# Layer norms of the MLP and of the image attention: the variance by one product with a matrix of ones, the reciprocal over all partitions

## The chip, the core and the metric

The kernel runs on one core of a Trainium2 chip. The time is the device time of one execution, in microseconds (us). The core has five engines that work side by side, each in the order of its own queue: PE (matrix products), DVE (elementwise work and reductions), ACT (functions of one argument, copies), POOL (elementwise work, a slower second one) and SP (issues DMAs). They wait for one another by semaphores. Products land in PSUM, which has eight banks of 128 partitions x 512 numbers; everything else lies in SBUF, 128 partitions wide.

## What is computed

Four images of 56 x 56 positions (L = 3136) and 128 channels pass four layers; each layer reads the group norm of x and is added to x. Layers 0 and 3 are the ones the change touches:

```python
x = x + _L0_conv_ref(_gn(x), ...)      # attention block
x = x + _L1_conv_ref(_gn(x), ...)      # selective scan
x = x + _L2_conv_ref(_gn(x), ...)      # deformable convolution
x = x + _L3_conv_ref(_gn(x), ...)      # attention block

# inside an attention block
attn_wins = _mha(wins, wq, bq, wk, bk, wv, bv, wo, bo)      # windows of 7 x 7
...
xf = xf + _mha(_layernorm(xf, g1, be1), wq, bq, wk, bk, wv, bv, wo, bo)
h = jax.nn.gelu(_layernorm(xf, g2, be2) @ w1 + b1, approximate=False)
xf = xf + (h @ w2 + b2)

def _layernorm(x, g, b, eps=1e-05):
    m = jnp.mean(x, axis=-1, keepdims=True)
    v = jnp.mean((x - m) ** 2, axis=-1, keepdims=True)
    return (x - m) * jax.lax.rsqrt(v + eps) * g + b
```

All of it is fp32. The two layer norms, over the 128 channels of each position, are the subject.

## The kernel before

Channels lie on the partitions and positions along the free axis, so an image is a tile of 128 x 3136. Work goes by chunks of 448 positions; an image has seven (NCK). One core does the four images one after the other, and each image has two attention blocks, so each stage below runs eight times. Inside these stages the order of the instructions is written out by hand: every engine takes its instructions in the order in which the loop issues them. The tiles' framework adds the waits and deals out the PSUM banks.

**The layer norm of a chunk.** A sum over channels is a sum over partitions, which is work for PE. `ln_center` (L140) multiplies the chunk by (identity - 1/128) and leaves the centred chunk in PSUM (`ln_pc`). ACT squares it into `ln_sq`. `ln_spread` (L150) takes the square in four pieces of 112 positions as the stationary side and a column of 1/128 as the moving side, so that the variances come out across 112 partitions, four to each (`ln_pv`); ACT takes the root of 112 x 4 numbers and DVE the reciprocal (`ln_rs`). `ln_rows` (L162) brings them back: four products of a broadcast column with the identity give 128 x 448 in PSUM, the same row in every partition (`ln_pb`), and ACT copies it to SBUF. DVE multiplies the centred chunk by it (`scale`), and ACT applies gain and bias (`shift`, an Identity). The scan's layer norm uses `ln_spread` too, with two halves of channels, and is not touched.

**First stage of the attention** (`attention`, loop over u = 0 to 8). The windowed attention of band u (tokens, project, queries, keys, values, scores, exponentials, normalize, turn, turned, weigh, out) is interleaved with the layer norm of chunk u - 2 and with `inputs`, which makes k, q and v of the image attention from it. Between them stand four calls of `some`, each four products of q with k (L349) and four maxima of them on DVE (L350) for the first four query blocks, if such work is ready. Of the names that the prediction uses: L302 is the eviction of `out`, L235 and L241 those of the queries (q) and keys (kb), L247 the copy of the values (v), L267 the exponential, L281 and L286 the transposes and their copies (turn, turned), L383 the square, L392 scale, L395 shift, L400 and L401 the products for k and q and their evictions. A pool of eight PSUM banks serves all of this.

**The image attention itself** (from L429 on) is long and not touched; its sums are inverted by L593, reciprocals of 128 x 112. It uses `one32`, a tile of ones of 128 x 32.

**The MLP** (`mlp`). Seven chunks again, in a loop over n from -1: `residual` (product with wo, L653, and DVE's add, L654), `center` (with POOL's add of x, L660), `spread`, `scale`, `shift`, `hidden` (four products, L679, and four Gelus, L680), `result` (four products, L686) and `store` (DVE's add, L690, then the statistics for the next group norm, L115, or in layer 3 `finish`, which sends the chunk out by DMA and fetches the next image's). In a turn, the norm of chunk n + 1 stands between the two halves of chunk n's `hidden`, and the residual of n + 2 follows. The pool has eight banks. Gelu, the root and the exponential lie in different function tables of ACT; a change of table is an instruction of its own (ACT_TABLE_LOAD).

Of the kernel before, what the change touches and what calls it, by code (L numbers as in the profile page):

```python
# [10 lines left out]
F32 = mybir.dt.float32  # L11
F32R = mybir.dt.float32r
I32 = mybir.dt.int32
AF = mybir.ActivationFunctionType
# [5 lines left out]
P = 128  # L20
HW = 56
L = HW * HW
CH = 448
NCK = L // CH
NH = 4
DK = P // NH
# [6 lines left out]
NPR = BAND // PW  # L33
# [37 lines left out]
def _offsets(cols):  # L71
    at, n = {}, 0
    for name, w in cols:
        at[name] = (n, w)
        n += w
    return at, n


class _Net:
    def __init__(self, ctx, tc, x, packs, out):  # L80
        self.tc, self.nc, self.x_in, self.out = tc, tc.nc, x, out
        self.B = x.shape[0]
        nc = self.nc
        wp = ctx.enter_context(tc.tile_pool(name="weights", bufs=1))
        self.keep = wp
        self.w = {}
        for i, (layer, cols) in enumerate(COLS.items()):
            at, n = _offsets(cols)
            t = wp.tile([P, n], F32, tag=f"w_{layer}", name=f"w_{layer}")
            (nc.sync if i % 2 == 0 else nc.scalar).dma_start(t, packs[layer])  # L90
            self.w[layer] = {name: t[:, o : o + k] for name, (o, k) in at.items()}
        c = self.w["C"]
        self.ident, self.gmat = c["ident"], c["gmat"]
        self.ones = {1: c["ones1"], 2: c["ones2"]}
        self.center = {1: (c["center1"],), 2: (c["center2"], c["others2"])}
        self.sel = wp.tile([P, KB], F32R, tag="sel", name="sel")
        nc.vector.memset(self.sel.bitcast(F32), 0.0)
        for h in range(NH):
            nc.vector.memset(self.sel[h * DK : h * DK + 2, :].bitcast(F32), 1.0)
        self.ident2 = wp.tile([64 + NX, NX], F32R, tag="ident2", name="ident2")  # L100
        nc.vector.memset(self.ident2.bitcast(F32), 0.0)
        for k in (0, 64):
            nc.vector.tensor_copy(self.ident2[k : k + NX, :], self.ident[:NX, :NX])
        self.one32 = wp.tile([P, DK], F32, tag="one32", name="one32")
        nc.vector.memset(self.one32, 1.0)
        self.eps = wp.tile([P, 1], F32, tag="eps", name="eps")
        nc.vector.memset(self.eps, 1e-5)
        self.x = wp.tile([P, L], F32, tag="x", name="x")
        self.st = wp.tile([P, NCK, 6], F32, tag="gn_st", name="gn_st")
        self.dpool = ctx.enter_context(tc.tile_pool(name="tables", bufs=1, space=DRAM))  # L110
# [51 lines left out]
    def ln_rows(self, dst, rs, bank):  # L162

        nc, k = self.nc, rs.shape[1]
        pb = bank("ln_pb")
        for i in range(k):
            nc.tensor.matmul(pb[:, i * QB : (i + 1) * QB], lhsT=rs[:, i : i + 1].to_broadcast([QB, P]), rhs=self.ident[:QB, :QB], start=True, stop=True)
        nc.scalar.copy(dst, pb[:, : k * QB])


    def swin_prepare(self, layer):
# [25 lines left out]
    def windows(self, layer, x, x1, gn, sb, bank):  # L197
# [5 lines left out]
        nc, w = self.nc, self.w[layer]  # L203
# [9 lines left out]
        def keep(name, t, shape):  # L213
            later[name, t] = sb.tile([P] + shape, F32, tag=name, name=name)
            return later[name, t]
# [27 lines left out]
        def values(t):  # L243
            pv = bank("pv")
            for r in range(NPR):
                nc.tensor.matmul(pv[:, r * P : (r + 1) * P], lhsT=xw[t % 2][:, 2 * r : 2 * r + 2, :].rearrange("p j k -> p (j k)"), rhs=w["wv"], start=True, stop=True)
            nc.vector.tensor_copy(keep("v", t, [NPR * P]), pv)  # L247

        def scores(t):
            s, m = keep("s", t, [ng, n1]), keep("m", t, [ng])  # L250
# [56 lines left out]
    def attention(self, layer, x, x1, oT, sb):  # L307
# [9 lines left out]
        nc, tc, w = self.nc, self.tc, self.w[layer]  # L317
# [8 lines left out]
        def part(c):  # L326
            return slice(c * CH, (c + 1) * CH)
# [12 lines left out]
        with tc.manual_schedule():  # L340
# [33 lines left out]
            with tc.tile_pool(name="ap_sb", bufs=2) as tb, tc.tile_pool(name="ap_ps", bufs=8, space=PSUM) as ps:  # L374
                bank = lambda name: ps.tile([P, 512], F32, tag="mm", name=name)
                of_windows = self.windows(layer, x, x1, self.group_norm(tb, ps), tb, bank)
                nc.gpsimd.memset(kl, 0.0)
                ln = {}
# [5 lines left out]
                    ln[c] = pc, sq  # L384

                def spread(c):
                    ln[c] += (self.ln_spread(ln[c][1][:, 0:1, :], bank, tb),)

                def scale(c):
                    pc, sq, rs = ln[c]  # L390
                    self.ln_rows(sq[:, 1, :], rs, bank)
                    nc.vector.tensor_mul(sq[:, 0, :], pc[:, :CH], sq[:, 1, :])  # L392

                def shift(c):
# [23 lines left out]
                def some():  # L418
                    if groups:
                        i, kc = groups.pop(0)  # L420
                        for h in range(NH):
                            maximum(i, h, kc, mx0[home[i][0]], bank, part(kc))

                def do(name, t):

                    if name in of_windows:
                        if 0 <= t < NWIN:
                            of_windows[name](t)
                    elif 0 <= t < NCK:  # L429
                        {"center": center, "spread": spread, "scale": scale, "shift": shift, "inputs": inputs}[name](t)  # L430

                for name in ("tokens", "project", "queries", "keys", "values"):
                    do(name, 0)
                do("tokens", 1)
                for u in range(NWIN + 1):
                    if u != 1:
                        do("scores", u)
                    do("out", u - 1)
                    some()
                    do("tokens", u + 2)  # L440
                    if u != 1:
                        do("exponentials", u)
                    do("center", u - 2)
                    if u != 1:
                        do("normalize", u)
                    do("project", u + 1)
                    do("spread", u - 2)
                    do("queries", u + 1)
                    do("values", u + 1)
                    if u == 0:  # L450
                        for name in ("keys", "scores", "exponentials", "normalize"):
                            do(name, 1)
                    some()
                    do("scale", u - 2)
                    if u != 0:
                        do("keys", u + 1)
                    some()
                    do("turn", u)
                    do("shift", u - 2)
                    do("turned", u)  # L460
                    do("inputs", u - 2)
                    some()
                    do("weigh", u)
# [10 lines left out]
            with tc.tile_pool(name="at_sb", bufs=2) as tb, tc.tile_pool(name="at_ps", bufs=2, space=PSUM) as ps:  # L474

                bank = lambda name: ps.tile([P, 512], F32, tag="mm", name=name, bufs=7)
# [123 lines left out]
                for g in range(ng + 8):  # L600
                    qc, k = divmod(g, NKB)
# [37 lines left out]
    def mlp(self, layer, x, x1, oT, last):  # L639


        nc, tc, w = self.nc, self.tc, self.w[layer]
        with tc.tile_pool(name="mlp", bufs=2) as sb, tc.tile_pool(name="mlp_ps", bufs=8, space=PSUM) as ps, tc.manual_schedule():
            bank = lambda name: ps.tile([P, 512], F32, tag="mm", name=name)
            x2, m = x1, {}

            def cols(n):
                c = (n + 3) % NCK
                return slice(c * CH, (c + 1) * CH)

            def residual(n):
                py = bank("py2")
                nc.tensor.matmul(py[:, :CH], lhsT=w["wo"], rhs=oT[:, n * CH : (n + 1) * CH], start=True, stop=True)  # L653
                nc.vector.scalar_tensor_tensor(x2[:, cols(n)], py[:, :CH], w["boe"], x1[:, cols(n)], ALU.add, ALU.add)  # L654

            def center(n):
                (m["pc", n],) = self.ln_center([x2[:, cols(n)]], bank)
                m["sq", n] = sb.tile([P, 2, CH], F32, tag="ln_sq", name="ln_sq")
                nc.scalar.activation(m["sq", n][:, 0, :], m["pc", n][:, :CH], AF.Square)
                nc.gpsimd.tensor_add(x2[:, cols(n)], x2[:, cols(n)], x[:, cols(n)])  # L660

            def spread(n):
                m["rs", n] = self.ln_spread(m["sq", n][:, 0:1, :], bank, sb)

            def scale(n):
                sq = m["sq", n]
                self.ln_rows(sq[:, 1, :], m.pop(("rs", n)), bank)
                nc.vector.tensor_mul(sq[:, 0, :], m.pop(("pc", n))[:, :CH], sq[:, 1, :])

            def shift(n):  # L670
# [25 lines left out]
            def do(f, n, *args):  # L696
                if 0 <= n < NCK:
                    f(n, *args)

            residual(0)  # L700
            for n in range(-1, NCK):
                do(center, n + 1)
                do(hidden, n, (0, 1))
                if n < 0:
                    residual(1)
                do(spread, n + 1)
                do(hidden, n, (2, 3))
                do(residual, n + 2 if n >= 0 else -1)
                do(scale, n + 1)
                do(result, n)  # L710
                do(shift, n + 1)
                do(store, n)


# [773 lines left out]
```

## Time and profile before

| | us |
|---|---|
| median of 3 timed runs | 13458.64 (13451.59 to 13462.05) |
| the profiled execution, its own time | 13245.72 |
| its span, first to last instruction | 13243.9 |
| mean granted PE clock | 0.933 |
| first stage of the attention, from the first scores (L257) to the eighth, first block | 29.50 to 150.69 |
| MLP, first L654 to last L690, eight of them | 69.56 to 74.65 |

The profiled execution is one run of its own, about 213 us below the timed median; durations are read from it. Of the operations that the change removes or alters, in the whole program:

| line, engine | operation | count | mean ns |
|---|---|---|---|
| L156 PE | variance, 128x112 by one column | 896 in the two norms (two records each product) | 237 (median) |
| L158 ACT | root, 112x4 | 140, with the scan's | 263 |
| L159 DVE | reciprocal, 112x4 | 140, with the scan's | 178 |
| L167 PE | back to rows, 112x112 | 896 | 298 |
| L168 ACT | copy, 128x448 | 112 | 532 |
| L247 DVE | copy of v, 128x512 | 64 | 684 |

A timeline line gives the start, the time that the merged instructions cover, the engine, the line, the operation with output and input, the count, and in brackets how long the engine stood idle before and what released it. PE works on an fp32 product in two records.

### The profile page before, as it was taken

The page shows a single profiled execution, that of the slowest core. Times are in us where ns is not written, and L with a number is a line of the kernel's source. Part 1 is how long each engine was busy: PE and PEld are TensorE (multiplying, and loading weights), DVE is VectorE, ACT ScalarE, POOL GpSimd, SP SyncE. Part 2 cuts the span into 40 slices and gives each one's busy share as a digit, 9 for nine tenths or more (in the row PEclk, how much of TensorE's full clock was granted, in tenths as well). Part 3 has the DMA queues.
Part 4 walks back from the last instruction along what each step waited for, and adds up shares of the span by engine and source line. Part 5 has one row for each costly group of instructions (what it writes and reads, how often), then busy time and mean ns, then how long its engine had stood idle before and what let it go on. Part 6 is the DMA issues. An engine that isn't in the chain of part 4 may idle for free. (4 is left out here: it accounts for less than half of the span.)

```text
span 13243.9 us, 218251 instructions
## 1 busy us (share of the span) xinstructions
PE 11713.7 (88%) x85716; PEld 7459.5 (56%) x85716; DVE 9575.5 (72%) x11831; ACT 7563.6 (57%) x19130; POOL 9941.6 (75%) x6852
## 2 busy tenths in 40 slices
PE   8999995699898999579989899957999989995799
PEld 4448884444544888444454488834445448883444
DVE  6649996665665999666466499966646649996664
ACT  5567772356556777235655677723565567772356
POOL 4949995488494999548849499954975949995497
PEclk9999997799999999779999999977999999996799
DMA  2000004200000000420000000042000000004200
GB/s 100 1 14 4 5 4 118 78 1 6 6 1 14 4 5 4 120 75 1 8 4 1 14 5 5 4 125 70 1 9 2 1 14 5 5 4 130 65 1 6
DMA packets 181178, 344.60 MB, mean 26 GB/s; under 512 B 20104, under 2 KB 101416, under 8 KB 180024
## 3 DMA queue, kind: packets, MB, share of 16 engines
q0 software_dynamic: 80640, 231.28, 6.3%
q1 hardware_dynamic: 99224, 97.83, 2.4%
q8 instruction: 678, 11.11, 0.4%
q14 instruction: 348, 2.85, 0.1%
q10 hardware_dynamic: 288, 1.53, 0.0%
HBM read 256.04 MB, written 74.52 MB: 25 GB/s over the span
## 5 line engine op out<-in xcount | busy, mean ns | idle before, releaser
L555 POOL TENSOR_TENSOR es<-es,e 128x896 f32<-128x896 f32 x2016 | 4158.8, 2088 | 133.0 <-ACT e L549 75.0
L350 DVE TENSOR_REDUCE mx<-pm 128x1 f32<-128x512 f32 (+1 forms) x4928 | 3056.5, 670 | 1411.1 <-PE pm L349 795.8
L549 ACT ACTIVATE e<-pst 128x448 f32<-128x448 f32 (+1 forms) x5600 | 2677.6, 544 | 1893.3 <-PE pst L547 1348.1
L1066 DVE TENSOR_TENSOR_SCAN hs<-da,dbu 128x928 f32<-128x928 f32 x1792 | 3633.0, 2070 | 53.2 <-ACT dbu L1059 29.3
L1075 POOL TENSOR_TENSOR hs<-hs,cb 128x896 f32<-128x896 f32 x1792 | 3486.9, 1963 | 26.0 <-ACT carry L1070 20.8
L349 PE MATMUL pm<-ks,qs 32*128 32x512 f32 (+1 forms) x9856 | 2911.8, 636 | 13.4 <-DVE nm L371 7.8
L547 PE MATMUL pst<-qs,ks 32*128 32x448 f32 x11200 | 2685.4, 547 | 0.0
L1084 PE MATMUL yt<-w_C,hs 128*116 128x128 f32 x14336 | 1865.8, 273 | 1.1 <-POOL hs L1075 1.1
L542 PE MATMUL pst<-nm,sel 32*128 32x448 f32 x5600 | 1638.7, 614 | 0.0
L1084 PEld LDWEIGHTS yt<-w_C,hs 128*116 128x116 f32 x14336 | 1570.5, 135 | 2.1 <-POOL hs L1075 2.1
L1048 PE MATMUL dbu<-dgb,ut 112*128 112x224 f32 x7168 | 1258.5, 298 | 268.8 <-DVE hs L1066 268.7
L571 PE MATMUL po<-e,va 128*32 128x448 f32 (+1 forms) x11200 | 1352.4, 551 | 0.1
L349 PEld LDWEIGHTS pm<-ks,qs 32*128 32x128 f32 x9856 | 924.3, 186 | 745.2 <-DVE mx L350 618.9
L1325 POOL DMA_INDIRECT g<-tab,idx x1008 | 940.5, 933 | 452.9 <-issue 425.8
L1048 PEld LDWEIGHTS dbu<-dgb,ut 112*128 112x128 f32 x7168 | 945.3, 192 | 534.2 <-DVE hs L1066 524.2
L1002 ACT ACTIVATE da<-dl,A 128x112 f32<-128x112 f32 x3584 | 1194.6, 383 | 0.1
L547 PEld LDWEIGHTS pst<-qs,ks 32*128 32x128 f32 x11200 | 1098.0, 185 | 102.6 <-issue 13.7
L1351 PE MATMUL pvt<-w_C,g 112*128 112x112 f32 x2016 | 404.5, 367 | 729.3 <-issue 607.8
L542 PEld LDWEIGHTS pst<-nm,sel 32*128 32x128 f32 x5600 | 570.6, 184 | 740.2 <-DVE mx L350 387.1
L1352 ACT COPY vt<-pvt 128x336 f32<-128x336 f32 x336 | 147.2, 438 | 1188.0 <-PE pvt L1351 1184.5
L1351 PEld LDWEIGHTS pvt<-w_C,g 112*128 112x128 f32 x2016 | 315.2, 203 | 823.1 <-issue 784.2
L1070 ACT COPY carry<-hs 128x32 f32<-128x32 f32 x1792 | 397.5, 222 | 623.3 <-DVE hs L1066 615.2
(230 smaller groups left out, 15791.4 us busy)
## 6 DMA issues: line engine op xcount, KB each, us to landing
tab<-zero SPq DMA_DIRECT2D x4, 6728.0 KB
g<-tab,idx POOLq DMA_INDIRECT x1008, 3.5
tab<-gt SPq DMA_DIRECT2D x32, 448.0 KB
dl_d<-dl SPq DMA_DIRECT2D x28, 448.0 KB
dl<-dl_d SPq DMA_DIRECT2D x56, 224.0 KB
tab<-gt SPq DMA_DIRECT2D x32, 336.0 KB
out_dram<-x SPq DMA_DIRECT2D x28, 224.0 KB
x<-in_x_dram SPq DMA_DIRECT2D x21, 224.0 KB
```

Of the source, the lines that this page charges most:

```text
L349: nc.tensor.matmul(pm[:, :m], lhsT=qs[head(h), q.start : q.start + P], rhs=ks[head(h), keys], start=True, stop=True)
L350: nc.vector.tensor_reduce(mx[:, home[i][1], h, kc : kc + 1], pm[:, :m], AX.X, ALU.max)
L542: nc.tensor.matmul(t[:, :CH], lhsT=self.sel[head(h), :], rhs=nm[head(h), part(qc)], start=True, stop=False)
L547: nc.tensor.matmul(t[:, :CH], lhsT=ks[head(h), k * KB : (k + 1) * KB], rhs=qs[head(h), part(qc)], start=False, stop=True)
L549: nc.scalar.activation(e[:nk, j, :], t[:nk, :CH], AF.Exp, scale=SCALE)
L555: nc.gpsimd.tensor_tensor(s, es[g - 1, p][:nk] if k == 1 else s, e[:nk], ALU.add)
L571: nc.tensor.matmul(m["po"][head(h), :CH], lhsT=va[:nk, k, head(h)], rhs=src(h)[:nk], start=(k == 0), stop=(k == NKB - 1))
L1002: nc.scalar.activation(m["da"][:, :, n, 2:], dl(), AF.Exp, scale=A[:, j, n : n + 1])
L1048: nc.tensor.matmul(pu[:, 8 * h : 8 * h + 8, 2 + tb * TB : 2 + (tb + 1) * TB], lhsT=made[g]["ut", 2 * r + tb][:, d, :], rhs=made["r", g // ...
L1066: nc.vector.tensor_tensor_scan(flat(pairs[u // 2][:, d % 2]), flat(made[g]["da"][:, r]), flat(banks.pop(u)), 0.0, ALU.mult, ALU.add)
L1075: nc.gpsimd.tensor_tensor(hs, hs, made["r", g // 2]["cb"][:, :, r * HW : (r + 1) * HW], ALU.mult)
L1084: nc.tensor.matmul(sums[q][:YR, e * P : (e + 1) * P], lhsT=hs[:, n, :], rhs=self.ident, start=(n == 0), stop=(n == NST // 2 - 1), is_trans ...
```

## The change

A tile of ones of 128 x 128 (`all1`) takes the place of `one32`, which becomes a slice of it. The new `ln_root` multiplies the square by it: one product of 128x128 by 128x448 puts the sum over channels of every position into every partition, and ACT takes the root of the whole 128 x 448 from PSUM, with 1/128 as scale and eps as bias. DVE then inverts 128 x 448 numbers. In the image attention this is in two halves (`invert0`, `invert1`) with a call of `some` between them, and the copy of v goes from DVE to ACT. In the MLP it is one reciprocal, and the loop's order is changed: centre, variance and reciprocal are a chunk further ahead, the residual two chunks further, and the first of these stand ahead of the loop.

```diff
-        self.one32 = wp.tile([P, DK], F32, tag="one32", name="one32")
-        nc.vector.memset(self.one32, 1.0)
+        self.all1 = wp.tile([P, P], F32, tag="all1", name="all1")
+        nc.vector.memset(self.all1, 1.0)
+        self.one32 = self.all1[:, :DK]
...
+    def ln_root(self, dst, sq, bank):
+
+        pv, k = bank("ln_pv"), sq.shape[-1]
+        self.nc.tensor.matmul(pv[:, :k], lhsT=self.all1, rhs=sq, start=True, stop=True)
+        self.nc.scalar.activation(dst, pv[:, :k], AF.Sqrt, bias=self.eps, scale=1.0 / P)
...
-            nc.vector.tensor_copy(keep("v", t, [NPR * P]), pv)
+            nc.scalar.copy(keep("v", t, [NPR * P]), pv)
...
                 def spread(c):
-                    ln[c] += (self.ln_spread(ln[c][1][:, 0:1, :], bank, tb),)
+                    sq = ln[c][1]
+                    self.ln_root(sq[:, 1, :], sq[:, 0, :], bank)
+
+                def invert(c, i):
+                    r = ln[c][1][:, 1, i * (CH // 2) : (i + 1) * (CH // 2)]
+                    nc.vector.reciprocal(r, r)
 
                 def scale(c):
-                    pc, sq, rs = ln[c]
-                    self.ln_rows(sq[:, 1, :], rs, bank)
+                    pc, sq = ln[c]
                     nc.vector.tensor_mul(sq[:, 0, :], pc[:, :CH], sq[:, 1, :])
...
                     do("spread", u - 2)
                     do("queries", u + 1)
                     do("values", u + 1)
+                    do("invert0", u - 2)
                     if u == 0:
                         for name in ("keys", "scores", "exponentials", "normalize"):
                             do(name, 1)
                     some()
+                    do("invert1", u - 2)
                     do("scale", u - 2)
...
             def spread(n):
-                m["rs", n] = self.ln_spread(m["sq", n][:, 0:1, :], bank, sb)
+                sq = m["sq", n]
+                self.ln_root(sq[:, 1, :], sq[:, 0, :], bank)
+                nc.vector.reciprocal(sq[:, 1, :], sq[:, 1, :])
 
             def scale(n):
                 sq = m["sq", n]
-                self.ln_rows(sq[:, 1, :], m.pop(("rs", n)), bank)
                 nc.vector.tensor_mul(sq[:, 0, :], m.pop(("pc", n))[:, :CH], sq[:, 1, :])
...
             residual(0)
+            residual(1)
+            center(0)
+            residual(2)
+            spread(0)
             for n in range(-1, NCK):
-                do(center, n + 1)
                 do(hidden, n, (0, 1))
-                if n < 0:
-                    residual(1)
-                do(spread, n + 1)
+                do(scale, n + 1)
+                do(center, n + 2)
                 do(hidden, n, (2, 3))
-                do(residual, n + 2 if n >= 0 else -1)
-                do(scale, n + 1)
+                do(shift, n + 1)
+                do(residual, n + 4)
+                do(spread, n + 2)
                 do(result, n)
-                do(shift, n + 1)
                 do(store, n)
```

More of the change, by code (lines that the diff above doesn't have):

```diff
@@ L429, in do @@
                     elif 0 <= t < NCK:
-                        {"center": center, "spread": spread, "scale": scale, "shift": shift, "inputs": inputs}[name](t)
+                        {
+                            "center": center, "spread": spread, "invert0": lambda c: invert(c, 0), "invert1": lambda c: invert(c, 1),
+                            "scale": scale, "shift": shift, "inputs": inputs,
+                        }[name](t)
                 for name in ("tokens", "project", "queries", "keys", "values"):
```

## The prediction

> **What bounds the kernel now.** I read the page's busy shares first, then the timelines of the two stages that the change touches, then the rows of single operations.
>
> ```profile
> PE 11713.7 (88%) x85716; PEld 7459.5 (56%) x85716; DVE 9575.5 (72%) x11831; ACT 7563.6 (57%) x19130; POOL 9941.6 (75%) x6852
> ```
>
> The share of PE is an average; the touched stages differ. There are eight of each: four images, two attention blocks (L0, L3). A turn of the MLP's loop, PE alone, in the timeline (start, duration, engine, line):
>
> ```profile
> 834.13 0.92 PE L147 MATMUL ln_pc<-x,w_C 128*128 128x448 f32 x2
> 834.88 1.67 PE L679 MATMUL ph<-xn,w_L 128*128 128x448 f32 x4
> ...
> 836.39 0.85 PE L156 MATMUL ln_pv<-w_C,ln_sq 128*112 128x1 f32 x8
> ...
> 837.10 1.75 PE L679 MATMUL ph<-xn,w_L 128*128 128x448 f32 x4
> ...
> 838.69 0.92 PE L653 MATMUL py<-oTi,w_L 128*128 128x448 f32 x2
> ...
> 839.44 1.04 PE L167 MATMUL ln_pb<-w_C,ln_rs 112*128 112x112 f32 x8
> ...
> 840.32 3.19 PE L686 MATMUL py<-h,w_L 128*128 128x448 f32 x8
> ...
> 843.34 0.92 PE L147 MATMUL ln_pc<-x,w_C 128*128 128x448 f32 x2
> ```
>
> PE never stops: 9.21 us a turn. Start to start, a 128x448 product (two records) takes 0.755, the eight short ones of L156 0.71, those of L167 0.88. So the MLP is bound by PE, and what leaves PE is gained.
>
> The image attention's first stage (loop over u = 0 to 8) is bound by a chain through all engines:
>
> ```profile
> 115.31 1.34 ACT L302 ACTIVATE x<-pwy,boe_L 128x196 f32<-128x196 f32 x6 [4.51 <-PE pwy L299]
> ...
> 120.56 0.26 ACT L158 ACTIVATE ln_rs<-ln_pv,eps 112x4 f32<-112x4 f32 x1
> 120.73 0.74 ACT L235 ACTIVATE qp<-pq,w_L 128x196 f32<-128x196 f32 x2
> 120.86 0.18 DVE L159 RECIPROCAL ln_rs<-ln_rs 112x4 f32<-112x4 f32 x1 [0.75 <-ACT ln_rs L158]
> ...
> 121.29 0.69 DVE L247 COPY v<-pv 128x512 f32<-128x512 f32 x1 [0.25 <-PE pv L246]
> ...
> 122.23 2.21 DVE L350 TENSOR_REDUCE mx<-pm 128x1 f32<-128x448 f32 x4 [0.25 <-PE pm L349]
> ...
> 123.33 0.53 ACT L168 COPY ln_sq<-ln_pb 128x448 f32<-128x448 f32 x1 [1.86 <-PE ln_pb L167]
> 123.75 2.37 ACT L241 ACTIVATE kb<-pk,w_L 32x392 f32<-32x392 f32 x4
> ...
> 126.14 0.76 ACT L395 ACTIVATE oTi<-ln_sq,w_L 128x448 f32<-128x448 f32 x1
> ...
> 126.96 1.02 PE L400 MATMUL apk<-oTi,w_L 128*128 128x448 f32 x2
> ```
>
> ACT works from 115.31 to 126.90 with one stop of 1.86; then PE makes k, q and v, the weighing and the next scores, and 19.83 us after the last one the next L302 begins (135.14). The end of L395 sets the turn. Two more rows, for the prices (min/median/max ns):
>
> ```profile
> L593 DVE RECIPROCAL rest<-rest x224: 793/836/854, 319.6 to 13164.7; 128x112 f32<-128x112 f32 x112
> L272 DVE RECIPROCAL m<-m x64: 252/253/254, 35.5 to 12521.4; 128x16 f32<-128x16 f32 x64
> ```
>
> **What the Trainium skill says.** "VectorE: DVE Perf Modes", *First, the fixed hardware budget*: reciprocal is an iterative divide with a repeat count of 8[...]. The trace agrees: 96 elements more cost 540 ns, 5.6 ns each, where the 448-element multiply of L392 takes 612 ns in all. "ScalarE: Activation LUTs", *What ACT_TABLE_LOAD costs*: a table load is about 1283 ns and a function costs the same per element as any other; the rows show L158's load at 1283 ns and L680's Gelu with a bias, 128x448 from PSUM, at 632. I price the wide root as that, 0.63. "TensorE: Matmul & The Clock Gate", *What's actually happening*: the clock halves when PE has been idle and returns after a window of about 3.4 us that is really busy. The trace: granted clock 0.50 from 804 to 820, although PE counts as busy from 812 on; the tiny products of L156 at 815 lie in that stretch.
>
> **The MLP, step by step.** A chunk's L156 and L167 (1.59 us of PE) become one product with ones, 0.755. The eviction L168 (0.53 ACT) goes, the root grows from 0.26 to 0.63, the reciprocal from 0.18 to .253 + 432 x 0.0056 = 2.68 us on DVE. Everything is also moved: center two chunks ahead, residual four, and more of both before the loop. In the loop PE has 11 wide products for n = 0 to 2, 10 for n = 3 and 4 (no residual left), 8 for n = 5 and 6: 3 x 8.30 + 2 x 7.55 + 2 x 6.04 = 52.1. Before: 5 x 9.21 + 8.46 + 6.04 = 60.55. Gain 8.45 an MLP at full clock.
>
> Is PE still the bound? ACT per turn: two loads 2.57, four Gelu 2.4, square 0.54, root 0.63, identity 0.76 = 6.9. The loop through DVE: reciprocal 2.7, behind it store's add 0.7 and statistics 0.63, then scale 0.63, identity 0.76, load 1.28, root 0.63, with handovers 7.6. So 8.30 holds and 7.55 just holds. The reciprocal is hidden by PE's work on the chunk before; without that cover it would cost 2.7 a chunk. The new wait is identity's for scale; behind it in ACT's queue stand only the table load and the root, counted in this loop. POOL's add of center (1.13 us) moves a chunk earlier on a queue that is idle 8 us a turn; store's DMAs keep their place and no DMA is added.
>
> The start before the loop: from the first L654 (802.57) to the first L679 (812.07) 9.5 us. New: add 0.6, three products in a row at half clock 3.9, root 0.63, reciprocal 2.7, scale 0.62, identity 0.76, handovers 0.3 = 9.5. Nothing. But these products (chunk 1's centre, more residuals) keep PE solidly busy from 803, so the full clock should be back before the loop. From first L654 to last L690 the eight MLPs take 69.6 to 74.65, mean 72.15, so half clock costs 2.6 over the best. I take 1.05 of this as gained: 9.5 an MLP, 76 us. Bounds: no clock gain and small losses 8.0, all of it 11.0.
>
> **The attention, step by step.** The v copy (0.69 DVE) becomes an ACT copy, about 0.5 to 0.6 by L286 (128x512). L167 and L168 go. Two half reciprocals of 253 + 208 x 5.6 = 1.42 us come, with four maxima reductions (2.13) between them. In turns u = 3 to 6 the path runs: root start 120.56, + 0.63, reciprocal 1.42, reductions 2.13, reciprocal 1.38 (its start overlaps), scale 0.61, handovers 0.1 = 126.83, against 126.14: +0.68 each, 2.7. ACT's root, q, v copy and kb end at 124.9 and wait; turned copies and the k, q, v evictions stand behind identity, and weigh waits for them. Other turns, by the same walk:
> - u = 0: the v copy stands in front of kb on ACT, and the second scores (37.60) wait for kb: +0.5.
> - u = 1: the copy must wait for PE's v product (ends 50.69), kb starts 51.25 instead of 49.90, and the turned copies follow: +1.35.
> - u = 2: no reductions are ready; kb, no longer behind L168, sets identity: 66.55 instead of 67.17, -0.6.
> - u = 7: PE was slow here with the short products and L168 ended at 163.2; -0.5.
> - u = 8: nothing else runs. Root 177.55, then the 6.2 of the DVE path: identity 183.75 instead of 181.31, +2.45.
>
> Sum +5.9 a stage, +47 us for eight. Bounds: 3.8 (copies overlap better) to 10 (reciprocals at POOL-busy length, PSUM waits of half a us a turn): +30 to +80.
>
> The wider memset of ones runs once, before the first x has landed: nothing, 0.1 us uncovered. The narrow ones are a slice of the wide tile: same shape on PE.
>
> **Sum.** -76 + 47 = -29 us on the profiled execution: 13245.7 to 13216.7. The timed runs' median lies 212.9 above the profiled one; I carry the difference over unchanged: 13430. Bounds of the likeliest case: -88 + 30 = -58 to -64 + 80 = +16, so 13400 to 13475.
>
> **Rivals.**
> A, more gain: the attention hides nearly all its reciprocals, since DVE is idle for 3.5 us ahead of the last reductions of a turn (130.60), and only u = 8 pays. For: that idle time. Against: it comes after identity, not before. -76 + 10 = -66: 13393.
> B, no change: the attention gives all back (9.5 a stage). For: POOL's L275 runs beside the first half reciprocal, and the centred product holds its PSUM bank until scale, so the fourth transpose bank comes late. Against: only about half a us of transposes hangs on it. 13459.
> C, slower: the MLP's eight banks. A turn now allots exactly eight; if they go round in turn, the centred product of n+2 takes the bank of n+1 and waits for its scale. The loop is then 3.0 of PE, product and root 2.8, reciprocal 2.7, store and statistics 1.3, scale 0.7 = 10.5 instead of 8.3, for four turns: about +9.2 an MLP, +74 - 29 = +45: 13504. It decides from about half of that wait. Against: before, nine were allotted a turn, and the result's product at 840.32 did not wait for the scale at 841.72 that round-robin would have made it wait for.
>
> **Numbers.** About 0.2%, 27 us, is what a measurement tells from no change. Likeliest 0.45 (0.25 of it beyond 27 faster, 0.17 within, 0.03 slower), A 0.22, B 0.18 (0.12 within, 0.06 slower), C 0.12, other 0.03. So faster 0.49, within 0.30, slower 0.21. The range leaves out most of C and the ends of A: 13385 to 13490.
>
> **What would show it.** MLP: L690 to L690 of 8.3 and 7.6 instead of 9.21, the reciprocal at 2.7, clock 1.00 by the first L679. Wrong if the centred product waits for DVE. Attention: stages 6 longer, with u = 8 the longest loss and identity ended by scale. Wrong if apk waits for a PSUM bank instead, or if a half reciprocal is far from 1.42.

## The result, and the profile after

The changed kernel takes 13485.35 us in the median of 13 runs (13474.10 to 13493.19), the kernel before 13462.05 beside it (13 runs, 13443.35 to 13479.08): ratio 1.0015, interval 1.0008 to 1.0023, so 23 us more, where 29 us less was forecast. The profiled execution of the changed kernel took 13474.1 by its own time, the lowest of its 13 runs.

First the engines' busy times, from its page:

```profile
PE 11613.8 (86%) x84148; PEld 7319.0 (54%) x84148; DVE 9832.2 (73%) x11823; ACT 7549.6 (56%) x19066; POOL 9942.8 (74%) x6852
```

PE has 100 us less to do, DVE 257 more. Which of the two decides is not the same in every stage. The table sums each kind of stage over its occurrences, from first and last rows of the traces; "before, again" is a second profile of the kernel before, which the experiments explain. The first stage of the attention runs from the group norm's statistics to the copy of the last keys, the MLP from the first residual add to the end of the last store.

| us in one execution | before | before, again | after |
|---|---|---|---|
| attention, first stage (8) | 1345.7 | 1352.1 | 1436.2 |
| image attention itself (8) | 4809 | 4811 | 4814 |
| MLP (8) | 582.7 | 584.4 | 504.4 |
| scan (4) | 4890.7 | 4889.8 | 4887.2 |
| deformable layer (4) | 1467.4 | 1688.3 | 1681.9 |
| span | 13243.9 | 13474.4 | 13472.3 |

The stretches between these stages, some 148 us in each of the three, are not in the table.

Two entries moved with the change: the MLP fell by 78 to 80 us, the first stage rose by 84 to 90. The sum is between +4 and +12; the timed runs say +23, with an interval from +11 to +31, so the two agree at the edge. A single profile can't do better: the eight first stages of the old attention alone came to between 1336.8 and 1352.1 in the five profiles that have them.

**The MLP.** Timeline of the same stretch as before the change, PE and what matters of DVE and ACT (start, duration, engine, line):

```profile
829.76 3.17 PE L703 MATMUL py<-h,w_L 128*128 128x448 f32 x8
...
831.72 2.95 DVE L681 RECIPROCAL ln_sq<-ln_sq 128x448 f32<-128x448 f32 x1 [1.82 <-ACT ln_sq L175]
...
832.77 1.67 PE L696 MATMUL ph<-xn,w_L 128*128 128x448 f32 x4
...
834.27 0.92 PE L148 MATMUL ln_pc<-x,w_C 128*128 128x448 f32 x2
...
835.02 1.67 PE L696 MATMUL ph<-xn,w_L 128*128 128x448 f32 x4
...
835.75 0.60 DVE L685 TENSOR_TENSOR ln_sq<-ln_pc,ln_sq 128x448 f32<-128x448 f32 x1
...
836.52 0.92 PE L669 MATMUL py<-oTi,w_L 128*128 128x448 f32 x2
...
837.26 0.75 ACT L689 ACTIVATE xn<-ln_sq,w_L 128x448 f32<-128x448 f32 x1
837.28 0.92 PE L174 MATMUL ln_pv<-ln_sq,all 128*128 128x448 f32 x2
...
838.03 3.17 PE L703 MATMUL py<-h,w_L 128*128 128x448 f32 x8
```

From L703 to L703 are 8.27 us, against 9.21 before, and PE's starts follow one another without a gap: eleven products at 0.75. The reciprocal runs from 831.72 to 834.67 beside PE's work on the chunk before it; its chain ends with the identity at 838.01, and the product that reads this comes at 841.03. It has 3 us to spare.

**The attention.** A turn from the middle of the first stage (u = 5, as is the turn in the prediction's lines), the path through ACT and DVE:

```profile
121.80 1.34 ACT L309 ACTIVATE x<-pwy,boe_L 128x196 f32<-128x196 f32 x6 [4.51 <-PE pwy L306]
...
127.06 0.63 ACT L175 ACTIVATE ln_sq<-ln_pv,eps 128x448 f32<-128x448 f32 x1
...
127.72 1.55 DVE L399 RECIPROCAL ln_sq<-ln_sq 128x224 f32<-128x224 f32 x1 [1.12 <-ACT ln_sq L175]
...
129.19 2.15 DVE L357 TENSOR_REDUCE mx<-pm 128x1 f32<-128x448 f32 x4
...
131.26 1.54 DVE L399 RECIPROCAL ln_sq<-ln_sq 128x224 f32<-128x224 f32 x1
...
132.83 0.62 DVE L403 TENSOR_TENSOR ln_sq<-ln_pc,ln_sq 128x448 f32<-128x448 f32 x1
...
133.49 0.76 ACT L406 ACTIVATE oTi<-ln_sq,w_L 128x448 f32<-128x448 f32 x1 [2.46 <-DVE ln_sq L403]
```

The identity begins 11.69 us after the eviction of `out` (133.49 - 121.80), where it was 10.83. In its bracket stands the new wait: ACT idles 2.46 us for DVE's scale, and DVE has been busy without a stop since 127.72 with half a reciprocal, the maxima and the other half.

Cut by the product of `out` that opens each turn (L299 before, L306 after), the first stage goes as follows, as means of its eight occurrences, next to the prediction's terms. The stretch up to the first of these products is u = 0, the one after the last of them u = 8.

| turn | before, us | after, us | measured | predicted |
|---|---|---|---|---|
| u = 0 | 28.53 | 28.92 | +0.4 | +0.5 |
| u = 1 | 11.05 | 13.82 | +2.8 | +1.35 |
| u = 2 | 18.29 | 18.06 | -0.2 | -0.6 |
| u = 3 to 6 | 77.61 | 80.99 | +3.4 | +2.7 |
| u = 7 | 18.33 | 19.40 | +1.1 | -0.5 |
| u = 8 | 14.41 | 18.35 | +3.9 | +2.45 |
| sum | 168.2 | 179.5 | +11.3 | +5.9 |

So the two parts were seen rightly in sign, the MLP in size as well, and the attention lost nearly twice what was forecast, which is enough to turn the forecast gain into a loss.

### The profile page after: what moved, and what is told of

It is laid out like the page before. It is cut to its first block, busy times and chain, and to the rows that moved or that the text cites. A ratio compares the mean times of both kernels' runs of the same rounds, so it can differ in the third digit from the quotient of the medians.

```text
span 13472.3 us, 215039 instructions
## 1 busy us (share of the span) xinstructions
PE 11613.8 (86%) x84148; PEld 7319.0 (54%) x84148; DVE 9832.2 (73%) x11823; ACT 7549.6 (56%) x19066; POOL 9942.8 (74%) x6852
## 5 line engine op out<-in xcount | busy, mean ns | idle before, releaser
L356 PE MATMUL pm<-ks,qs 32*128 32x512 f32 (+1 forms) x9856 | 2944.4, 633 | 29.1 <-DVE mx L357 15.8
L282 POOL TENSOR_TENSOR pz<-s,m 64x784 f32<-64x784 f32 x128 | 191.8, 1498 | 803.2 <-DVE m L279 798.7
```

Of the source, the lines that this page charges most:

```text
L356: nc.tensor.matmul(pm[:, :m], lhsT=qs[head(h), q.start : q.start + P], rhs=ks[head(h), keys], start=True, stop=True)
```

## The experiments

All times are medians of timed runs, with the ratio to the kernel before on the same chip, unless a single run is named. The theory throughout is the one of the table: the MLP gains about 78 us, the attention loses about 87. "Half clock" is time in which the granted PE clock of the profile is 0.50.

**Where the 213 us of the first profile went.** The kernel before, profiled once more, nothing edited.

> The kernel before, unchanged, profiled once more. The two profiles differ by 214 us in the deformable layer (1467 us over four images before, 1682 after), more than in all else, while the timed medians differ by 23 us. Theory: that layer's time belongs to the single execution, and the first profile of before was an odd one; then this profile has about 1680 us in the deformable layer and a time near 13460, with the other stages as in the first profile. Rival: the change slows that layer by 214 us and something outside the profile makes up for it; then this one has 1467 again and a time near 13245.

A single run: 13476.21 us, span 13474.4. The row of the deformable layer's gathers, in the groups of instructions (busy time and mean, then the idle time of POOL before them and what ended it), first profile of before:

```profile
L1325 POOL DMA_INDIRECT g<-tab,idx x1008 | 940.5, 933 | 452.9 <-issue 425.8 <-DMA g<-tab,idx 25.3 <-DVE g L1340 0.6
```

and the second:

```profile
L1325 POOL DMA_INDIRECT g<-tab,idx x1008 | 940.3, 933 | 612.4 <-issue 439.6 <-remote 109.5 <-PE pvt L1351 45.9
```

The same 1008 gathers, as long as before (933 ns each), and 160 us more of idle time between them. The table of stages shows where the first profile was short: 221 us in the deformable layer, which the change doesn't touch. A later set of runs on another chip had the kernel before at a median of 13232.74 and, in profiles of two other kernels, this layer at 1459 and 1463. So this layer's time goes with the chip on which a set of runs was made, and the first profile fits that other chip; the offset doesn't come from the profiling. Whether the chip itself is the reason, or something else that differed between the sets of runs, was not tested.

**One part alone.** The new MLP with the old attention (`mlp_only`), and the new attention with the old MLP (`attn_only`). The edits put the old loop back in the one or in the other place, for instance

```diff
                 def spread(c):
-                    sq = ln[c][1]
-                    self.ln_root(sq[:, 1, :], sq[:, 0, :], bank)
+                    ln[c] += (self.ln_spread(ln[c][1][:, 0:1, :], bank, tb),)
...
-                    do("invert0", u - 2)
...
-                    do("invert1", u - 2)
```

> The MLP's part of the change alone, the attention as before. Theory: the stages' differences add up: the eight MLPs lose 78 us (582.7 to 504.4 in the profiles) and nothing else moves, so 13462 - 78 = 13384, ratio 0.994, and an MLP takes 63 us from its first residual. Rival: the MLP's gain hangs on what stands ahead of it, or is given back in the next stage; then the ratio is nearer to 1 than 0.996.

> The attention's part of the change alone, the MLP as before. Theory: its first stage loses 11.3 us each time (168.2 to 179.5 from group norm to the copy of the last keys), 90 us for eight, so 13552, ratio 1.0067. Rival: a part of these 90 us comes from the MLP's part, by another state of the PE clock at the stage's start; then under 60 us, ratio below 1.0045.

`mlp_only`: 13384.17, ratio 0.9940 (0.9926 to 0.9954), 75 us less. `attn_only`: 13543.08, ratio 1.0062 (1.0048 to 1.0075), 84 us more. In its trace the first stages sum to 1429.5, turn by turn within 0.6 us of the changed kernel's. The parts are what the table says they are, and they nearly cancel: together +9, where the changed kernel's own +23 lies within what these two intervals leave open (each some 18 us to either side).

**Arithmetic or order in the MLP.** `mlp_old_order` keeps the old attention, has the product with ones, the wide root and the reciprocal in the MLP, and the old order of the loop. The cut shows its loop against the changed kernel's.

```diff
             residual(0)
-            residual(1)
-            center(0)
-            residual(2)
-            spread(0)
             for n in range(-1, NCK):
+                do(center, n + 1)
                 do(hidden, n, (0, 1))
-                do(scale, n + 1)
-                do(center, n + 2)
+                if n < 0:
+                    residual(1)
+                do(spread, n + 1)
...
```

> The MLP's new arithmetic (one product with ones, root and reciprocal over all partitions) in the old order of the loop; the attention as before. Theory: one chunk ahead is too little: root, reciprocal of 2.9 us, the residual's add and scale come after the Gelus of a turn, and the hidden products of the next chunk wait for them, 9.2 to 10 us a turn instead of 8.3, an MLP of 69 to 75 us; within 20 us of before, 13445 to 13480. Rival: the 0.84 us that PE saves a turn is the gain, whatever the order; then an MLP of 66 to 67, 13405 to 13415.

13449.44, ratio 0.9996 (0.9988 to 1.0005); the MLP's stages sum to 585.5 us, against 584.4. From its timeline, a turn:

```profile
824.23 2.95 DVE L672 RECIPROCAL ln_sq<-ln_sq 128x448 f32<-128x448 f32 x1 [3.45 <-ACT ln_sq L175]
...
827.60 0.61 DVE L676 TENSOR_TENSOR ln_sq<-ln_pc,ln_sq 128x448 f32<-128x448 f32 x1
...
828.25 0.76 ACT L680 ACTIVATE xn<-ln_sq,w_L 128x448 f32<-128x448 f32 x1 [1.58 <-DVE ln_sq L676]
...
829.07 1.77 PE L687 MATMUL ph<-xn,w_L 128*128 128x448 f32 x4 [0.31 <-ACT xn L680]
...
833.49 2.95 DVE L672 RECIPROCAL ln_sq<-ln_sq 128x448 f32<-128x448 f32 x1 [4.02 <-ACT ln_sq L175]
```

The turn is 9.26 us (833.49 - 824.23), though PE has only eleven products in it. `hidden` waits for the identity, this for the scale, this for the reciprocal, and all of them lie within one turn. The cheaper arithmetic alone gains nothing; only with the chain a chunk ahead does PE set the pace. The reverse, the old arithmetic in the new order, was not run. The prediction's lines leave it little to gain inside the loop, since PE there goes from product to product for all of the 9.21 us.

**The reciprocals in the attention.** `no_recip` leaves out both half reciprocals of the image attention's norm and keeps everything else.

```diff
                 def invert(c, i):
                     r = ln[c][1][:, 1, i * (CH // 2) : (i + 1) * (CH // 2)]
-                    nc.vector.reciprocal(r, r)
+                    pass
```

> The change, with the two half reciprocals of the attention's layer norm left out (the chunk is multiplied by the root instead of its inverse; the MLP is as changed). Theory: they lie on the path from the root to the identity, so in the middle turns (20.0 to 20.7 us) identity comes 2.1 to 2.5 earlier, until ACT's kb ends it, and turn 8 (18.35) loses 3.1 or more; -13 to -17 us a stage, 13350 to 13380. Rival: they are mostly hidden and the stage lost its 11 us by the v copy, the PSUM banks and the PE clock; then less than -5 us a stage, above 13445.

13372.06, ratio 0.9939 (0.9924 to 0.9955), first stages 1335.8. Its middle turn, timeline of ACT and DVE:

```profile
120.57 0.63 ACT L175 ACTIVATE ln_sq<-ln_pv,eps 128x448 f32<-128x448 f32 x1
...
124.33 0.61 DVE L403 TENSOR_TENSOR ln_sq<-ln_pc,ln_sq 128x448 f32<-128x448 f32 x1
...
124.98 0.76 ACT L406 ACTIVATE oTi<-ln_sq,w_L 128x448 f32<-128x448 f32 x1 [0.43 <-DVE ln_sq L403]
```

Root to identity takes 4.41 us, in the changed kernel 6.43, and the 2.46 us of ACT's wait are down to 0.43. The turns u = 3 to 8 take 18.24, 18.26, 18.93, 18.26, 16.69 and 14.85: the reciprocals cost 2.0, 1.8, 1.8, 1.8, 2.7 and 3.5 us of the changed kernel's. u = 1 stays at 13.49, so its loss has another cause. A stage is 12.5 us shorter than in the changed kernel, just short of the forecast 13 to 17, and the eight together take about what the old attention takes (1336.8 to 1352.1): the reciprocals are worth the attention's whole loss.

**The copy of v.** `v_on_dve` gives all copies of v back to DVE, `v_split`, whose edit is shown, only the first three.

```diff
-            nc.scalar.copy(keep("v", t, [NPR * P]), pv)
+            (nc.vector.tensor_copy if t < 3 else nc.scalar.copy)(keep("v", t, [NPR * P]), pv)
```

> The change with the copy of v put back on DVE, all else as changed. Theory: in turn u = 1 (and u = 0) the copy's place in ACT's queue ahead of kb is what costs 3.2 us a stage, part of it by half clock that follows; in turns 3 to 6 the copy on DVE stands ahead of the first half reciprocal and its 0.69 us lie on the path. So the first steps fall back to 28.5 and 11 us, the four middle turns rise by 0.5 to 0.7 each, and the sum is between -2 and +1 us a stage, -16 to +8 us in all. Rival: the copy on ACT is hidden and u = 1 is slow for another cause; then the first steps stay at 28.9 and 13.8 and the sum is +20 us or more.

> The change, with the first three copies of v (those issued ahead of and in turns 0 and 1) on DVE and the later ones on ACT. Theory: only the early copies stand in the way on ACT, and only the late ones would on DVE; so the second step falls from 13.8 to 11.3 and the others stay (18.1, 20.3, 20.0, 20.7, 20.0, 19.4), -2 to -3.5 us a stage, 13457 to 13470. Rival: the gain in the first steps is handed on as a loss to the next turns, as in the run with all copies on DVE; then 13480 or more.

`v_on_dve`: 13497.09, ratio 1.0029 (1.0019 to 1.0040). u = 1 falls to 11.25 as expected, but the middle turns rise by 0.6 each, u = 2 to 19.08 and u = 3 to 22.44, with 3.4 us at half clock in u = 3. The expectation missed that last part: by the timed runs the kernel is 12 to 19 us slower than the changed one, above its band of -16 to +8, though the first stages of the profile are only 5.7 longer. `v_split`: 13461.35, ratio 1.0004 (0.9996 to 1.0012), u = 1 at 11.06, u = 4 to 7 as in the changed kernel to 0.01 us. Its first stages sum to 1422.4, 14 less, a little under the 16 to 28 that were expected, not least because u = 0 is 1.1 longer. The copy on ACT is what costs u = 1, and is right in the middle of the stage. The changed kernel's u = 1, timeline:

```profile
51.29 1.05 PE L253 MATMUL pv<-w_L,xw 128*128 128x128 f32 x8
...
52.44 0.59 ACT L254 COPY v<-pv 128x512 f32<-128x512 f32 x1 [1.30 <-PE pv L253]
...
52.92 2.40 ACT L248 ACTIVATE kb<-pk,w_L 32x392 f32<-32x392 f32 x4
...
55.98 1.89 PE L301 MATMUL pwo<-at,v 128*32 128x128 f32 x32 [1.89 <-ACT at L293]
57.81 4.60 PE L264 MATMUL pss<-kb,qp 128*128 128x196 f32 x16
```

and the kernel before, same place:

```profile
49.90 2.41 ACT L241 ACTIVATE kb<-pk,w_L 32x392 f32<-32x392 f32 x4 [0.29 <-PE pk L230]
...
52.97 1.89 PE L294 MATMUL pwo<-at,v 128*32 128x128 f32 x32 [0.53 <-ACT at L286]
54.79 2.92 PE L257 MATMUL pss<-kb,qp 128*128 128x196 f32 x16
```

ACT waits 1.30 us for PE's v, and `kb` stands behind that copy: it starts 5.40 us after the turn began, 4.03 before. That is the forecast 1.35. PE then idles 1.89 instead of 0.53 before the weighing, and the scores after it run at half clock: 4.60 us for what took 2.92. That 1.7 was not in the forecast.

**Both halves in front of the maxima.** `invert_first` moves `invert1` up beside `invert0`.

```diff
                     do("invert0", u - 2)
+                    do("invert1", u - 2)
...
                     some()
-                    do("invert1", u - 2)
                     do("scale", u - 2)
```

> The change, with both half reciprocals issued ahead of the four maxima instead of one on each side. Theory: the path from root to identity holds the maxima (2.15 us) too, so without them turn 8 loses 2.1 of its 18.35; in the middle turns identity gains up to 2.1, less what the transposes then wait for banks that the undone maxima hold, so 0.5 to 1.5 a turn; -4 to -8 us a stage, 13420 to 13455. Rival: it is the sum of DVE's work in a turn that sets the turn, and the order is of no account: middle turns and turn 8 within 0.3, 13478 to 13492.

13511.43, ratio 1.0045 (1.0031 to 1.0059): slower than the changed kernel, which neither theory had. The middle turns come in two lengths. Of the eight turns u = 5, four have no half clock and take 20.5 us, 0.2 less than the changed kernel's; four have 3.4 us of it and take 21.9. One of each in the timeline, first with half clock:

```profile
128.68 2.96 DVE L399 RECIPROCAL ln_sq<-ln_sq 128x224 f32<-128x224 f32 x2 [1.12 <-ACT ln_sq L175]
...
133.28 3.43 PE L288 MATMUL pt<-w_C,pz 128*128 128x128 f32 x16
...
134.28 0.76 ACT L406 ACTIVATE oTi<-ln_sq,w_L 128x448 f32<-128x448 f32 x1 [2.28 <-DVE ln_sq L403]
...
136.55 0.92 PE L411 MATMUL apk<-oTi,w_L 128*128 128x448 f32 x2
```

then without, in the second stage:

```profile
2640.20 1.97 PE L288 MATMUL pt<-w_C,pz 128*128 128x128 f32 x16
...
2641.35 0.76 ACT L406 ACTIVATE oTi<-ln_sq,w_L 128x448 f32<-128x448 f32 x1 [2.29 <-DVE ln_sq L403]
...
2642.16 1.02 PE L411 MATMUL apk<-oTi,w_L 128*128 128x448 f32 x2
```

Identity comes 6.26 us after the root in both (128.02 and 2635.09), 0.2 sooner than in the changed kernel. But at half clock the transposes take 3.43 instead of 1.97 us, and the product for k, behind them on PE, begins 1.5 us after the identity's end at 135.04; without half clock it follows at once. A stage has 40.7 us at half clock where the changed kernel's has 28.7, and what is more lies nearly all in u = 4 to 8: u = 7 takes 21.84, and 12.8 us of u = 8 are at half clock. A window of 3.4 us at half clock makes the turn u = 4 longer by 1.4 us (21.3 instead of 19.9); at that rate the twelve us more would cost an estimated 4.9, and the stage is 4.8 longer. So the loss is the clock's and not the path's. That the maxima between the halves keep PE busy enough for the full clock fits this, but which pause on PE tips the clock was not tested; the prediction had not considered it.

**The half clock of the last turn.** In `warm_last` four products whose results nobody reads stand in the last turn's gap on PE. They add work and change nothing else.

```diff
                     some()
+                    if u == NWIN:
+                        pf = bank("pf")
+                        for _ in range(4):
+                            nc.tensor.matmul(pf[:, :CH], lhsT=self.all1, rhs=x1[:, part(0)], start=True, stop=True)
                     do("turn", u)
```

> The change, with four wide products more in the last turn of the attention's first stage, ahead of the products for k and q; their result is read by nobody. PE is idle there for 3.5 us while DVE inverts. Theory: a part of what the last turn lost is half clock that follows this idle time (9.4 us of it in that step, 5.5 to 7.2 before); with PE busy the products for k, q and v come at full clock, the step falls from 18.35 to 16.3 to 17.2, and the time is 13468 to 13478. Rival: the last turn is long by the reciprocals alone and the clock there is its consequence without a price; the step stays within 0.3 of 18.35 and the time within 13480 to 13492.

13248.84, ratio 1.0009 (1.0001 to 1.0017), on the chip where before takes 13232.74. The last turn falls from 18.35 to 17.20, at the edge of what was expected, and its time at half clock from 9.4 to 5.1 us. First the changed kernel without these products, timeline of its first u = 8:

```profile
192.07 0.76 ACT L406 ACTIVATE oTi<-ln_sq,w_L 128x448 f32<-128x448 f32 x1 [5.80 <-DVE ln_sq L403]
...
192.89 1.86 PE L411 MATMUL apk<-oTi,w_L 128*128 128x448 f32 x2 [3.48 <-ACT oTi L406]
194.54 1.70 PE L411 MATMUL apq<-oTi,w_L 128*128 128x448 f32 x2
...
196.03 2.08 PE L417 MATMUL apv<-w_L,oTi 128*128 128x128 f32 x8
```

then with them, its second:

```profile
2639.57 4.97 PE L477 MATMUL pf<-x,all 128*128 128x448 f32 x8
2644.38 0.92 PE L411 MATMUL apk<-oTi,w_L 128*128 128x448 f32 x2
2645.13 0.91 PE L411 MATMUL apq<-oTi,w_L 128*128 128x448 f32 x2
2645.88 1.19 PE L417 MATMUL apv<-w_L,oTi 128*128 128x128 f32 x8
```

With PE idle for 3.48 us, the products for k, q and v take 5.2 us (192.89 to 198.11); with the gap filled, 2.7 (2644.38 to 2647.07). But the kernel before had a part of this too. The same products in its first u = 8:

```profile
182.12 1.51 PE L400 MATMUL apk<-oTi,w_L 128*128 128x448 f32 x2 [1.37 <-ACT oTi L395]
...
183.42 1.70 PE L400 MATMUL apq<-oTi,w_L 128*128 128x448 f32 x2
...
184.91 1.69 PE L406 MATMUL apv<-w_L,oTi 128*128 128x128 f32 x8
```

They take 4.5 us (182.12 to 186.60), after a pause of only 1.37. Over its eight stages they take 2.8 three times and 4.1 to 4.7 five times, mean 3.9; in the changed kernel 4.7 to 5.2 all eight times, mean 4.8. The filling itself ran mostly at half clock, 4.97 us where it took 3.27 in the first stage, so that it ended late: the product for k began 14.60 us after the turn's `out`, in the changed kernel's second stage 13.34, which gives half of the gain back. In the other turns the profile of this run is longer (14.25 in u = 1), and the ratio's interval overlaps the changed kernel's: the half clock is shown to be a part of the last turn's length, a faster kernel is not.

**The version that beats both.** `mlp_only` once more, on that other chip.

> The version that the runs point to, once more beside the others on one chip: the MLP's part of the change with the attention as before. Theory: 13384 again, ratio 0.994. Rival: the first reading was a chip's; then a ratio outside of 0.9926 to 0.9954.

13157.67 against 13232.74: ratio 0.9940 (0.9927 to 0.9954), the same as on the first chip. The new MLP with the old attention is 0.6% faster than before, and 0.75% faster than the change (0.9940/1.0015).

## Why the prediction was right and wrong

**The MLP, -76: right**, measured -78 to -80. Its two terms are both there. "Gain 8.45 an MLP at full clock": the shortest MLP before is 70.25 us, after 61.73, 8.5 less, and neither has half clock behind the first product of `hidden`. The wait of the identity on DVE is hidden, as walked, and `mlp_old_order` shows what it costs without that cover: the whole gain. The reciprocal was priced at 2.68 and takes 2.95, which stays hidden too. The 1.05 for the clock came out somewhat larger, 9.8 to 10.0 an MLP less 8.5, or 1.3 to 1.5. Its reason is not shown. Time at half clock in an MLP fell from 11.1 to 3.0 us, but in `attn_only`, whose MLP is the old one, it was 6.0, and its eight MLPs summed to 565.9 instead of 584.4. Nor did the sign that the prediction named, "clock 1.00 by the first L679", come true in more than one MLP of eight: in the others the first 2.8 to 3.4 us behind that product are at half clock, though ahead of it half clock is nearly gone (0.6 us at most, 1.7 to 8.4 before). The term's size so owes something to luck. What precedes the MLP matters to its clock as well, as `attn_only` shows, and how much of the gain is due to the moved products stays open. Rival C, PSUM banks in turn, is out: PE has no gap in the loop. That its 13504, slower, lies nearest to the 13485 that were measured is luck.

**The attention, +47: the step that failed**, by size: 11.3 a stage where the sum "+5.9 a stage" stood. Four of its terms were too small, and u = 2 gave back 0.2 instead of 0.6.

- "Two half reciprocals of 253 + 208 x 5.6 = 1.42 us": they take 1.55. The row of the prices had 793/836/854 for 112 elements, and the working took 793, the minimum; with the median, 836, the slope is 6.1 ns and the half 1.52. It makes the middle turns +0.85 each instead of +0.68.
- "u = 1: +1.35": the wait is there, but the pause that it leaves on PE costs the clock of the scores, 1.7 us more.
- "u = 7: -0.5": the eight stages of the kernel before took 19.6 us in this turn four times and 16.7 to 18.0 four times; the one that was read belonged to the slower four, and its granted clock was 0.83 there. The changed kernel takes 19.40 in all eight, with or without half clock in them, because ACT waits 5.80 us for DVE before the identity (at 173.76 in the first stage). Without reciprocals it is 16.69, the same as before without half clock. So the turn was judged against a disturbed baseline, and the reciprocals were given no cost in it at all.
- "u = 8: +2.45": the walk itself is right, the identity comes 2.77 later after `out` than before in the first stage (11.02 instead of 8.25), 3.0 in the mean of the eight. The other 1.0 of the +3.9 is the clock's: behind PE's pause of 3.48 us the last products run mostly at half clock in all eight stages, in the kernel before in five. `warm_last` got 1.15 back.

Three of these four have the clock in them, which the prediction read for the MLP and not for the attention. The Trainium skill, "TensorE: Matmul & The Clock Gate", *What's actually happening*, has the activity watched in free-running windows of about 3.4 us. The traces agree: the time at half clock in a turn is nearly always a multiple of that, 3.41, 6.83 or 10.24 us in turns 1, 7 and 8 of the changed kernel. But PE need not have been idle for the clock to halve, which is how the prediction put it: ahead of the half clock in the scores of u = 1 (at 58.00 us) PE counted as busy for 54% of a window, ahead of that in the first u = 8 of the kernel before (at 182.52) for 60%. So a pause is not paid by its length alone: in `warm_last` the products for k, q and v take 2.7 us, behind the pause of 3.48 us they take 4.8. Of each of the eight first stages, 21.8 us were at half clock before (23.7 in the second profile), 28.7 after.

**The rivals.** A, the attention hides nearly all, is out. B had the attention give the whole gain back, at 9.5 a stage, and comes nearest in size. But its mechanism, transposes late for want of a bank, is not what happened: in the middle turns the product for k begins 0.05 us after the identity's end. Nor did POOL's work lengthen the half reciprocals: they take 1.54 us without it and 1.55 beside it.

**The offset of 212.9 us**, carried over unchanged, did no harm to the difference: it lies in the deformable layer, which the change doesn't touch. From the forecast to the result are 55 us: 3 of them are the drift of the kernel before between the two sets of runs (13458.64 to 13462.05), 37 to 43 the attention's term (84 to 90 instead of 47), and the MLP's term takes off 2 to 4. Some 15 us are left, which the profiles don't place, and which are as large as the spread of the old attention's first stages over five profiles.

## What to carry to other kernels

Work that leaves the bounding engine is gained only if what replaces it lies outside the turn's chain; the same new arithmetic was worth 0.6% with the norm a chunk ahead and nothing in the old order, and in a stage bound by a chain through DVE it cost 0.6%. When a wait is added in front of matrix products, price the pause on PE too, since the products after it may run at half clock. Read the turn that a price is set against in every occurrence of the stage, and take the price of an operation from the median of a row, of a size as near to its own as there is.

## What the runs showed that was not expected

Rows of the changed kernel's tile `ln_sq` (min/median/max ns):

```profile
L175 ACT ACTIVATE ln_sq<-ln_pv,eps x112: 613/633/634, 67.2 to 13455.2; 128x448 f32<-128x448 f32 x112
L399 DVE RECIPROCAL ln_sq<-ln_sq x112: 1494/1548/1554, 67.8 to 12782.8; 128x224 f32<-128x224 f32 x112
...
L681 DVE RECIPROCAL ln_sq<-ln_sq x56: 2952/2953/2954, 819.9 to 13455.9; 128x448 f32<-128x448 f32 x56
```

DVE's reciprocal costs 6.3 ns for each further element, (2953 - 1548)/224, where ACT's root of the same tile takes 633 ns in all. In each trace, half clock begins only on a grid of 3.41 us that is kept from the first window to the last. In the first stages of the changed kernel, of the windows at full clock in which PE counted as busy for less than 40%, all 8 were followed by half clock; of those with 40 to 70%, 31 of 78; of those with more, none of 260. Over all twelve profiles these are 124 of 124, 250 of 735 and 13 of 3249. So a stretch in which PE is busy about half of the time can go either way, and the same turn then comes in several lengths.

And the kernel before differs by 1.7% between the runs on two chips (13462 and 13233 us for the same code), nearly all of it in the deformable layer, which is about ten times what this change did.
